# Layer 2 attention in steps of three score tiles and three quarter runs of values

## The chip, the core and the metric

The kernel runs on one core of a Trainium2 chip. A core has TensorE (matrix products into PSUM, the accumulator memory; the profile calls it PE and its weight loads PEld), VectorE (DVE), ScalarE (ACT), GpSimd (POOL) and SyncE (SP, which issues DMA transfers). Each engine takes its instructions in a fixed order, and semaphores make one engine wait for another. So the order that is built into the program decides who waits for whom. The metric is the device time of one execution in microseconds (us).

## The reference

Four layers, each an attention over a context and a feed-forward part, act on x of shape 4 x 256 x 256 (batch, tokens, width). Layer 2's attention is the part that matters here. It has 16 query heads of 128, four heads to each of 4 key/value groups, and keys of two origins: 1601 context keys and the 256 tokens themselves, the latter under a causal mask.

```
q = (x @ wq).reshape(B, L, NUM_HEADS, HEAD_DIM)
k = (x @ wk)...; v = (x @ wv)...            # 4 groups, repeated for their 4 heads
k_ctx = rms_norm(h_ctx_kv @ wk_ctx ...); v_ctx = h_ctx_kv @ wv_ctx ...
q, k = rms_norm + rotary embedding
scores = jnp.einsum('blhd,bmhd->bhlm', q, k_full) * scale + mask
probs = jax.nn.softmax(scores, axis=-1)
out = jnp.einsum('bhlm,bmhd->blhd', probs, v_full)
return out.reshape(B, L, NUM_HEADS * HEAD_DIM) @ wo
```

## The kernel before

**Units, heads, tiles.** `l2_xattn` (L1361) works through 16 units, one for each batch and key/value group, with 4 heads in each: 64 heads. The context's keys and values were projected earlier and are loaded for each unit (`prep`, L1452). A head's 256 queries are cut into 8 groups of 32, and two groups make a score tile. So a head has four score tiles, c = 0 to 3, and the layer has 256.

**Scores** (`scores`, L1549). The stationary side is 32 queries, so four matmuls work side by side on quarters of the array (128x32 weights), each over a quarter of the keys; a tile has eight such fours, of 416, 448 or 480 columns (causality makes later groups longer). In the trace every fp32 matmul is two passes. The tile lies in PSUM in one of three buffers of two banks (`ps_s`, L1375). VectorE adds the mask and takes the row maximum, ScalarE takes the exponential with the row sum into an SBUF tile p (8 buffers, L1560).

**Softmax of a head.** A row's keys lie in four quarters of the partitions, each with its own maximum and sum. `merge` (L1578) gathers these (GpSimd, ms), forms shares on VectorE and ScalarE (lo, em, wm, tot), and GpSimd writes the factors (rm). `scale` (L1603) multiplies p by them with eight GpSimd instructions. `turn` (L1611) transposes p on VectorE into pT (two buffers), in blocks of 32.

**Values** (`values`, L1618). For each of 15 blocks of keys one matmul with full 128x128 weights adds into o (256 columns), and after the last block ScalarE copies o to `at` (L1627). o has one buffer (`ps_o`, L1377). `CHUNK` (L1638) cuts the 15 into runs of 4, 4, 4 and 3.

**Side work.** `prep` of the next unit is a generator whose pieces are: two query projections (tpq, two matmuls of 512 columns each, read by ScalarE's square and VectorE's two products), keys and values of the tokens (tpkv), the norm's factors (two loads of ScalarE's table), two rounds of transposes of the queries (tpqT) and one of the keys (tpk). `project` (L1629) multiplies a unit's four heads by wo (acc, 16 passes). tpq, tpkv, tpqT, tpk and acc share one PSUM buffer (`ps`, L1376).

**Order.** The loop at L1677 makes steps of two score tiles, eight to a unit. A step issues two tiles, a part of the previous head's softmax, and half of the values (two runs) of the head before that; the tables `WHEN` and `BETWEEN` (L1674, L1675) say how many pieces of `prep` go into each step, and `project` of the last unit comes in step 7. The tile framework's scheduler then sets the order of each engine's instructions, except those that `pin` (L165) keeps in the order of the program: the transposes and the first sum of a merge. `mm` (L116) calls `ordered`, which pins a matmul only while `self.strict` is set; in this layer it is not.

Of the kernel before, what the change touches and what calls it, by code (L numbers as in the profile page):

```python
# [11 lines left out]
F32 = mybir.dt.float32  # L12
# [6 lines left out]
AF = mybir.ActivationFunctionType  # L19
ALU = mybir.AluOpType  # L20
# [77 lines left out]
class Kernel:  # L98
# [1262 lines left out]
    def l2_xattn(self):  # L1361
# [10 lines left out]
        with ExitStack() as es:  # L1372
# [28 lines left out]
            def turned(b):  # L1401

                xn = self.xn.tile([P, 2, D], F32, name="xn")
                if b:
                    self.layernorm(xn, self.x[b])
                    exps_next()
                else:

                    mv = self.small.tile([P, 2, 2], F32, name="ln_mv")
                    for q in range(2):  # L1410
                        st = self.small.tile([P, 6], F32, name="st3")
                        nc.vector.bn_stats(st, self.x[b][:, q, :])
                        nc.vector.bn_aggr(mv[:, q, :], st)
                    r = self.small.tile([P, 8], F32, name="ln_r8", bufs=1)
                    self.root(r[:, :2], mv[:, :, 1], 1.0, 1e-5, r[:, 2:])
                    for q in range(2):
                        nc.vector.tensor_scalar(
                            xn[:, q, :], self.x[b][:, q, :], mv[:, q, 0:1], r[:, q : q + 1],
                            ALU.subtract, ALU.mult,
                        )  # L1420
                    self.fill(LN2)
                tp = ps.tile([P, 2, 2, P], F32, name="tp_ln", tag="tp")
                for k in range(2):
                    for q in range(2):
                        nc.tensor.transpose(tp[:, k, q, :], xn[:, q, k * P : (k + 1) * P], self.ident)
                t = self.xnT.tile([P, 2, S], F32, name="xT2", tag="xnT")
                nc.scalar.copy(t, tp.rearrange("p k q t -> p k (q t)"))
                return t
# [18 lines left out]
            def load_out(g):  # L1447
                t = two.tile([P, 4, D], F32, name="wo")
                nc.sync.dma_start(t, i["l2_wo"][g])
                return t  # L1450

            def prep(u, w, res):  # L1452
# [75 lines left out]
                    yield  # L1528
                tp = ps.tile([P, 4, P], F32, name="tpk", tag="tp")
                for m in range(2):  # L1530
                    nc.tensor.transpose(tp[:, m, :], ko[:, m, :], self.ident)
                c = CT * P + 96
                nc.gpsimd.memset(kT[:, NK - 1, 96:], 0.0)
                nc.scalar.copy(
# [11 lines left out]
                n0, n1 = tiles_of(2 * c), tiles_of(2 * c + 1)  # L1546
                return [(0, 2, n0)] if n0 == n1 else [(0, 1, n0), (1, 2, n1)]

            def scores(kT, qT, h, c, ms):  # L1549

                s = ps_s.tile([P, 2, 512], F32, name="s2")
                for n in range(2):
                    q0 = (2 * c + n) * 32
                    nt = tiles_of(2 * c + n)
                    for a in range(4):
                        self.mm(
                            s[32 * a : 32 * a + 32, n, : nt * 32].rearrange("p (t i) -> p t i", i=32),
                            qT[:, h, q0 : q0 + 32], kT[:, :nt, 32 * a : 32 * a + 32], True, True,
                        )
                p = main.tile([P, 2, NK * 32], F32, name="p2", bufs=8)  # L1560
                for n0, n1, nt in spans(c):
                    e0, e1 = 2 * c + n0, 2 * c + n1
                    sv = s[:, n0:n1, CT * 32 : nt * 32]
                    nc.vector.tensor_tensor(  # L1564
                        sv, sv, mask[:, e0:e1, : nt - CT, :].rearrange("p n t i -> p n (t i)"), ALU.add
                    )
                    nc.vector.tensor_reduce(  # L1567
                        ms[:, 0, e0:e1], s[:, n0:n1, : nt * 32], AX.X, ALU.max, negate=True
                    )
                    for n in range(n0, n1):  # L1570
                        e = 2 * c + n
                        nc.scalar.activation(  # L1572
                            p[:, n, : nt * 32], s[:, n, : nt * 32], AF.Exp, bias=ms[:, 0, e : e + 1],
                            accum_out=ms[:, 1, e : e + 1],
                        )
                return p

            def merge(ms):  # L1578

                c = self.small.tile([32, 4, 2, 8], F32, name="ms2")
                for a in range(4):
                    nc.gpsimd.tensor_copy(c[:, a], ms[32 * a : 32 * a + 32])
# [4 lines left out]
                e = self.small.tile([32, 4, 8], F32, name="em2")  # L1589
                nc.vector.tensor_tensor(e, wide(lo), c[:, :, 0], ALU.subtract)  # L1590
                nc.scalar.activation(e, e, AF.Exp)
                yield
                w = self.small.tile([32, 4, 8], F32, name="wm2")
                nc.vector.tensor_tensor(w, e, c[:, :, 1], ALU.mult)
                tot = self.small.tile([32, 8], F32, name="tot2")
# [4 lines left out]
                    nc.gpsimd.tensor_tensor(r[32 * a : 32 * a + 32], e[:, a], tot, ALU.mult)  # L1600
                return r

            def scale(p, r, c):  # L1603
                for n in range(2):
                    e = 2 * c + n
                    nt = tiles_of(e)
                    nc.gpsimd.tensor_scalar(  # L1607
                        p[:, n, : nt * 32], p[:, n, : nt * 32], r[:, e : e + 1], 1.0, ALU.mult, ALU.mult
                    )

            def turn(p, pT, c):  # L1611
                for n0, n1, nt in spans(c):
# [24 lines left out]
            ORDER = [0, 13, 14, *range(1, NM)]  # L1637
            CHUNK = [ORDER[0:4], ORDER[4:8], ORDER[8:12], ORDER[12:]]  # L1638

            def softmax_steps(hd):  # L1640


                shares = merge(hd["ms"])
                next(shares)
                yield
                r = yield from shares
                hd["pT"] = main.tile([P, 8, NK, 32], F32, name="pT2")
                for c in range(4):
                    scale(hd["p"][c], r, c)
                yield  # L1650
                for c in range(4):
                    turn(hd["p"][c], hd["pT"], c)
                yield

            def value_steps(hd):
                o = ps_o.tile([P, S], F32, name="o2")
                for n, ms in enumerate(CHUNK):
                    values(hd["va"], hd["pT"], hd["at"], hd["h"], o, ms)
                    if n % 2:
                        yield  # L1660

            units = [(b, g) for b in range(B) for g in range(NKV2)]
            w = load(0)
# [3 lines left out]
                self.fill(Q2 if n == 0 else C2 if n == 3 else 0)  # L1667
            for _ in self.early:
                pass
            self.es2.close()  # L1670
            main = es.enter_context(tc.tile_pool(name="a2main", bufs=2, side="right", reuse_waits="tile"))


            WHEN = [0, 1, 1, 1, 1, 1, 1, 0]  # L1674
            BETWEEN = [0, 0, 0, 0, 0, 0, 1, 0]  # L1675
            soft = vals = hd = None
            for n, (b, g) in enumerate(units):  # L1677
                kT, va, qT = ready
                last = hd
                ready, pieces = [], None  # L1680
                wo_now = wo
                at = main.tile([P, 4, S], F32, name="at2", bufs=2)
                for h in range(4):
                    hd = {"ms": self.small.tile([P, 2, 8], F32, name="nmsm2"), "p": [], "va": va, "at": at, "h": h, "b": b,
                          "wo": wo_now}
                    for c in (0, 2):
                        step = 2 * h + c // 2
                        for cc in (c, c + 1):
                            hd["p"].append(scores(kT, qT, h, cc, hd["ms"]))
                        if soft is not None:  # L1690
                            next(soft[0])
                        if pieces is not None:
                            for _ in range(BETWEEN[step]):
                                next(pieces, None)
                        if vals is not None:
                            next(vals)
                        if step == 0 and n + 1 < len(units):
                            b1, g1 = units[n + 1]
                            w = load(g1)
                            pieces = prep(n + 1, w, ready)  # L1700
                            if g1 == 0:
                                next(pieces)
                        if step == 4 and n + 1 < len(units):
                            wo = load_out(g1)
                        if pieces is not None:
                            for _ in range(WHEN[step]):
                                next(pieces, None)
                        if step == 7 and last is not None:
                            project(last)
                        if soft is not None and c == 0:  # L1710
                            next(soft[0])
                    vals = value_steps(soft[1]) if soft is not None else None
                    soft = (softmax_steps(hd), hd)
                if pieces is not None:
                    for _ in pieces:
                        pass
            for n in range(2):
                next(soft[0])
                next(vals)
                if n == 0:  # L1720
                    next(soft[0])
            for _ in value_steps(hd):
                pass
            project(hd)


    def l3_open(self, es):

# [759 lines left out]
```

## Time and profile before

| what | us |
|---|---|
| median of 3 runs (lowest, highest) | 2390.23 (2389.08, 2396.24) |
| the profiled execution | 2387.69 |
| its span, from first to last instruction | 2386.0 |
| layer 2 attention in it, first scores to end of the last projection | 691.1 to 1689.6 |
| all score matmuls of that layer, TensorE busy | 424.2 |
| all value matmuls of that layer, TensorE busy | 431.7 |

The profile's durations come from the one profiled execution, whose own time is 1.7 us over its span. Matmuls are pipelined: a row's mean duration is longer than the distance from one start to the next, so costs on TensorE are read from starts, or from the chain of waits, which gives each stretch its share of time without overlap. The columns of a group are: line, engine, operation, output <- inputs, shapes, count, then busy time and mean of one in ns, then the idle time of the engine just ahead of them and who ended it.

### The profile page before, as it was taken

The numbers are of one execution on the slowest core, as the hardware profiler recorded it, in microseconds if no ns is written. First come the engines' busy times: TensorE is split into PE (matmuls) and PEld (weight loads), VectorE is DVE, ScalarE is ACT, GpSimd is POOL, SyncE is SP. The second block draws the span as 40 slices with busy tenths as digits, with TensorE's granted clock in tenths as the row PEclk, the third lists the DMA queues.
The fourth block names the chain that finished last, engine by engine and source line by source line (L and its number), as shares of the span: only waits on it lengthen the run. The fifth ranks groups of instructions, "written<-read, shape, count | busy, mean of one in ns | idle before, by whom it ended". The sixth has DMA issues, their size and how long they took to land.

```text
span 2386.0 us, 42230 instructions
## 1 busy us (share of the span) xinstructions
PE 2255.6 (95%) x14335; PEld 1382.2 (58%) x14335; DVE 1473.2 (62%) x3553; ACT 1272.4 (53%) x2877; POOL 948.7 (40%) x1707
## 2 busy tenths in 40 slices
PE   8989997889989999999999999999899889999996
PEld 5677875777745555555555655555665533444332
DVE  5453532773457777777777777777334574758344
ACT  3334443552474555555555555553232577888994
POOL 1014655503335544555554555554121253334220
PEclk9989998989999999999999999999899999999998
DMA  7165575652550111111111111100534353434320
GB/s 267 41 201 161 172 156 157 197 185 65 167 179 32 43 51 47 47 51 51 51 52 51 51 51 50 44 10 10 205 124 117 114 156 103 109 94 103 83 64 19
DMA packets 156078, 234.47 MB, mean 98 GB/s; under 512 B 33929, under 2 KB 122761, under 8 KB 154666
## 3 DMA queue, kind: packets, MB, share of 16 engines
q1 hardware_dynamic: 138998, 190.07, 25.0%
q0 software_dynamic: 11280, 31.60, 5.4%
q10 hardware_dynamic: 5588, 10.09, 1.4%
q8 instruction: 117, 1.92, 0.3%
q14 instruction: 95, 0.78, 0.1%
HBM read 169.94 MB, written 61.74 MB: 97 GB/s over the span
## 4 chain that ended last, share of the span: by engine, by line
PE 78%; DVE 7%; issue 5%; DMA 4%; ACT 2%; POOL 2%; SPq 1%; ACTq 0%; POOLq 0%; DVEq 0%
PE o L117 17%; PE s L117 17%; PE o L77 6%; PE b L77 3%; PE f2gu L117 3%; PE s L77 3%; PE f1gu L117 2%; PE fill L1307 2%; PE f0gu L117 2%; PE acc L117 2%; PE tpq L117 2%; PE av L117 2%; PE f0y L117 2%; PE f2y L117 1%; PE f1y L117 1%
## 5 line engine op out<-in xcount | busy, mean ns | idle before, releaser
L1572 ACT ACTIVATE p<-s,nmsm 128x448 f32<-128x448 f32 (+2 forms) x512 | 324.7, 639 | 369.6 <-DVE nmsm L1567 317.4
L117 PE MATMUL o<-pT,va 128*128 128x256 f32 (+2 forms) x1920 | 431.7, 377 | 3.3 <-DVE pT L1613 2.9
L117 PE MATMUL s<-kT,qT 128*32 128x448 f32 (+2 forms) x4096 | 424.2, 550 | 4.2 <-ACT p L1572 4.2
L77 ACT ACTIVATE e<-s 128x1024 f32<-128x1024 f32 (+1 forms) x416 | 392.4, 1041 | 57.4 <-PE s L77 56.3
L117 PEld LDWEIGHTS o<-pT,va 128*128 128x128 f32 (+1 forms) x1920 | 344.7, 190 | 127.9 <-issue 75.4
L1607 POOL TENSOR_SCALAR p<-p,rm 128x448 f32<-128x448 f32 (+2 forms) x512 | 320.7, 649 | 6.3
L1567 DVE TENSOR_REDUCE nmsm<-s 128x1 f32<-128x448 f32 (+4 forms) x384 | 293.2, 783 | 4.4
L1613 DVE STREAM_TRANSPOSE pT<-p 128x448 f32<-128x448 f32 (+4 forms) x384 | 278.1, 778 | 11.1 <-POOL p L1607 11.1
L117 PEld LDWEIGHTS s<-kT,qT 128*32 128x32 f32 x4096 | 121.7, 109 | 250.2 <-issue 213.9
L77 PE MATMUL o<-e,va 128*32 128x512 f32 x1656 | 246.9, 614 | 12.3 <-DVE os L77 12.2
L1600 POOL TENSOR_TENSOR rm<-em,tot 32x8 f32<-32x8 f32 x256 | 50.3, 197 | 335.6 <-DVE tot L1597 303.3
L1564 DVE TENSOR_TENSOR s<-s,mask 128x64 f32<-128x64 f32 (+4 forms) x384 | 92.5, 260 | 128.5 <-PE s L117 82.4
L77 PEld LDWEIGHTS s<-qb,kb 32*128 32x128 f32 (+1 forms) x1664 | 65.5, 180 | 182.3 <-issue 143.7
L1307 PE MATMUL fill<-wkc_early,ctxT 128*128 128x256 f32 (+1 forms) x444 | 110.5, 401 | 8.9 <-ACT va_early L1315 6.7
L522 POOL DMA_INDIRECT f0xr<-f0xd,f0src x95 | 91.3, 961 | 66.5 <-PE f0y L117 25.5
L77 PE MATMUL s<-qb,kb 32*128 32x256 f32 (+1 forms) x1664 | 111.5, 331 | 3.1 <-ACT e L77 1.8
L77 POOL CAST kb<-kf 128x384 fp32r<-128x384 f32 (+1 forms) x126 | 65.5, 549 | 96.4 <-PE s L77 61.8
L1307 PEld LDWEIGHTS fill<-wkc_early,ctxT 128*128 128x128 f32 (+1 forms) x444 | 87.0, 200 | 25.3 <-ACT va_early L1315 7.8
L1572 ACT ACTIVATION_READ_ACCUMULATOR p<-s,nmsm 128x1 f32 x512 | 100.5, 196 | 0.0
L1326 DVE TENSOR_REDUCE ss_early<-sq_early 128x4 f32<-128x512 f32 x64 | 37.1, 580 | 82.8 <-ACT sq_early L1325 72.0
L630 POOL DMA_INDIRECT f0yt<-f0yd,f0slot x64 | 63.1, 987 | 60.7 <-DVE x L622 29.8
L117 PE MATMUL f2gu<-f2wgu,f2xsT 128*128 x176 | 85.1, 608 | 0.6 <-ACT f2xsT L114 0.3
(579 smaller groups left out, 3689.2 us busy)
## 6 DMA issues: line engine op xcount, KB each, us to landing
kf<-kd SPq DMA_DIRECT2D x384, 48.0 KB
vd<-va_early SPq DMA_DIRECT2D x96, 128.0 KB
kd<-kT_early SPq DMA_DIRECT2D x48, 256.0 KB
kT<-kd SPq DMA_DIRECT2D x16, 768.0 KB
va<-vd SPq DMA_DIRECT2D x16, 768.0 KB
kd<-kt SPq DMA_DIRECT2D x96, 128.0 KB
f0yd<-f0ys SPq DMA_DIRECT2D x95, 128.0 KB
ctxT<-in_ctxT SPq DMA_DIRECT2D x5, 1664.0 KB
```

The costliest lines, as they stand in the source:

```text
L77: ins = f(*a, **kw)
L117: self.ordered(self.nc.tensor.matmul(out, lhsT, rhs, start=start, stop=stop, **kw))
L522: nc.gpsimd.indirect_dma_start(out=t, out_offset=None, in_=xd[:, :], in_offset=bass.IndirectOffsetOnAxis(ap=src[:, n : n + 1], axis=0),)
L630: nc.gpsimd.indirect_dma_start(out=yt, out_offset=None, in_=yd[:, :], in_offset=bass.IndirectOffsetOnAxis(ap=slot[:, t, r : r + 1], axis=0),)
L1307: ins = nc.tensor.matmul(tp[:rows, t, :], ctxT[u // NKV2][:, k, c0 : c0 + rows], w[u % NKV2][:, k, :], start=k == 0, stop=k == 1,)
L1326: nc.vector.tensor_reduce(ss[:, m0:m1], sq[:, : m1 - m0, :], AX.X, ALU.add)
L1564: nc.vector.tensor_tensor(sv, sv, mask[:, e0:e1, : nt - CT, :].rearrange("p n t i -> p n (t i)"), ALU.add)
L1567: nc.vector.tensor_reduce(ms[:, 0, e0:e1], s[:, n0:n1, : nt * 32], AX.X, ALU.max, negate=True)
L1572: nc.scalar.activation(p[:, n, : nt * 32], s[:, n, : nt * 32], AF.Exp, bias=ms[:, 0, e : e + 1], accum_out=ms[:, 1, e : e + 1],)
L1600: nc.gpsimd.tensor_tensor(r[32 * a : 32 * a + 32], e[:, a], tot, ALU.mult)
L1607: nc.gpsimd.tensor_scalar(p[:, n, : nt * 32], p[:, n, : nt * 32], r[:, e : e + 1], 1.0, ALU.mult, ALU.mult)
L1613: self.pin(nc.vector.transpose(pT[:, 2 * c + n0 : 2 * c + n1, :nt, :].rearrange("p n t i -> p n (t i)"), p[:, n0:n1, : nt * 32],))
```

## The change

The loop over units, heads and pairs of tiles becomes one flat loop over the 256 score tiles, three to a step. Tile x belongs to unit x // 16 and head x // 4; k = x % 16 is its place in the unit.

- A step first issues the scores of three tiles; mask, maximum and exponential are a function of their own (`weights`), called for the first two tiles, and for the third after the first run of values.
- Then follow three positions. Position x issues a quarter run of the values that lies nine tiles back (`LATE` = 9), and then `beside`, the side work of that place: `PIECES` puts tpq at k = 0 and 4, tpkv at 6, the norm at 7, tpqT at 10 and 12, tpk at 13; `project` is at k = 8, the loads of wo at 9 and of the next but one unit's wq and wks at 13.
- Heads whose last tile was in the step have merge and scaling issued at its end, and their transposes after the first run of values of the next step.
- `self.strict` is set for the loop, so TensorE keeps the order of the program; transposes tp_ln and tpk are ordered too.
- p has 9 buffers instead of 8. The last head's scaling is shared between GpSimd and ScalarE.

What is computed does not change, nor do the number and shapes of the matmuls.

```diff
-            def scores(kT, qT, h, c, ms):
+            def scores(kT, qT, h, c):
...
+                return s
+
+            def weights(s, c, ms):
+
+                p = main.tile([P, 2, NK * 32], F32, name="p2", bufs=9)
...
-            def scale(p, r, c):
+            def scale(p, r, c, shared):
                 for n in range(2):
                     e = 2 * c + n
                     nt = tiles_of(e)
+                    v = p[:, n, : nt * 32]
+                    if shared and n:
+                        nc.scalar.activation(v, v, AF.Copy, scale=r[:, e : e + 1])
+                    else:
+                        nc.gpsimd.tensor_scalar(v, v, r[:, e : e + 1], 1.0, ALU.mult, ALU.mult)
...
+            w = load(1)
...
-            WHEN = [0, 1, 1, 1, 1, 1, 1, 0]
-            BETWEEN = [0, 0, 0, 0, 0, 0, 1, 0]
...
+            PIECES = {0: 1, 4: 1, 6: 1, 7: 1, 10: 1, 12: 1, 13: 9}
+            heads, turning, pieces = [], [], None
...
+            def beside(n, k):
+
+                nonlocal w, wo, pieces
+                if k == 8 and n:
+                    project(heads[4 * n - 1])
+                if n + 1 == len(units):
+                    return
+                b1, g1 = units[n + 1]
+                if k == 0:
+                    pieces = prep(n + 1, w, ready)
+                for _ in range(1 if k == 2 and g1 == 0 else PIECES.get(k, 0)):
+                    next(pieces, None)
+                if k == 9:
+                    wo = load_out(g1)
+                if k == 13 and n + 2 < len(units):
+                    w = load(units[n + 2][1])
...
+            self.strict = True
+            LATE, ALL = 9, 16 * len(units)
+            for i0 in range(0, ALL + LATE, 3):
+                run = range(i0, min(i0 + 3, ALL))
+                made = []
+                for x in run:
+                    n, h, c = x // 16, x // 4 % 4, x % 4
+                    if x % 16 == 0:
+                        begin(n)
+                    hd = heads[x // 4]
+                    if c == 0:
+                        hd["ms"] = self.small.tile([P, 2, 8], F32, name="nmsm2")
+                    made.append((hd, c, scores(hd["kT"], hd["qT"], h, c)))
...
+                soften(slice(0, 2))
+                for pos in range(3):
+                    x = i0 + pos
+                    if LATE <= x < ALL + LATE:
+                        value_chunk(heads[(x - LATE) // 4], (x - LATE) % 4)
+                    if pos == 0:
+                        soften(slice(2, 3))
+                    if x < ALL:
+                        beside(x // 16, x % 16)
+                    if pos == 0:
+                        for hd in turning:
+                            turns(hd)
+                        turning = []
+                for hd, c, _ in made:
+                    if c == 3:
+                        softmax(hd, hd is heads[-1] and len(heads) == 4 * len(units))
+                        turning.append(hd)
+            project(heads[-1])
+            self.strict = False
```

## The prediction

> **What bounds the kernel now.** I read the page first, then the busy time of the engines over three stretches of the layer 2 attention, then the chain inside one unit of it, then the rows of its side engines.
>
> ```profile
> span 2386.0 us, 42230 instructions
> PE 2255.6 (95%) x14335; PEld 1382.2 (58%) x14335; DVE 1473.2 (62%) x3553; ACT 1272.4 (53%) x2877; POOL 948.7 (40%) x1707
> ```
> ```profile
> core 0: us, PE busy (x) PEld busy (x) DVE busy (x) ACT busy (x) POOL busy (x), PEclk, DMA share, GB/s
> 691.07:718.95 27.88, 23.66 (x183) 7.23 (x182) 21.42 (x48) 19.91 (x50) 10.33 (x24) 0.93 0.24 83
> 718.95:1663.60 944.65, 943.87 (x6383) 552.34 (x6382) 728.80 (x1582) 489.58 (x1364) 485.88 (x1083) 1.00 0.13 44
> 1663.60:1689.60 26.00, 23.37 (x109) 19.50 (x106) 12.50 (x22) 3.64 (x12) 10.25 (x22) 1.00 0.00 1
> ```
>
> From 718.95 us (first values) to 1663.60 (last scores) TensorE is idle for 0.8 us of 945, at a granted clock of 1.00. Layer 2 attention is bound by TensorE's own queue; VectorE is next with 77%, ScalarE has 52%, GpSimd 51%. The page's chain gives values and scores 17% of the span each. What TensorE does inside one unit:
>
> ```profile
> 1029.34 3.31 PE s L117 x32
> 1032.65 3.22 PE o L117 x14
> 1035.87 0.44 PE tpqT L1526 x4
> 1036.30 3.09 PE s L117 x32
> 1039.39 0.59 PE tpqT L1526 x4
> 1039.98 0.03 issue
> 1040.02 3.46 PE o L117 x16
> 1043.48 0.22 PE tpk L1531 x2
> 1043.70 3.30 PE s L117 x32
> 1047.00 3.22 PE o L117 x14
> 1050.22 3.45 PE acc L117 x16
> ```
>
> (start, length, work; a matmul is two passes.) Read three things. The 16 passes of acc take 3.45 us, 0.216 each, so 14 value passes should take 3.02; after scores they take 3.22. Second, the second tpqT takes 0.59 where the first took 0.44, then 0.03 and a slower run: TensorE waits for the transposes pT of VectorE, about 0.27 us a unit. Third, a unit repeats every 62.0 us (the same tpqT stands at 977.35 and 1039.32). The rows that take part in the new steps:
>
> ```profile
> L1572 ACT ACTIVATE p<-s,nmsm 128x448 f32<-128x448 f32 (+2 forms) x512 | 324.7, 639 | 369.6 <-DVE nmsm L1567 317.4
> L1607 POOL TENSOR_SCALAR p<-p,rm 128x448 f32<-128x448 f32 (+2 forms) x512 | 320.7, 649 | 6.3
> L1567 DVE TENSOR_REDUCE nmsm<-s 128x1 f32<-128x448 f32 (+4 forms) x384 | 293.2, 783 | 4.4
> L1613 DVE STREAM_TRANSPOSE pT<-p 128x448 f32<-128x448 f32 (+4 forms) x384 | 278.1, 778 | 11.1 <-POOL p L1607 11.1
> ```
> ```profile
> L1627 ACT COPY at<-o x64: 366/370/378, 729.0 to 1686.7; 128x256 f32<-128x256 f32 x64
> ```
>
> The last one empties the only value buffer (min/median/max ns). Today nothing on TensorE waits for it: a score block of 3.1 us stands between a head's last values and the next head's first.
>
> **The change, part by part.** The order of instructions on each engine is read from the two programs, every time from the rows.
>
> *Fewer changes between scores and values (gain).* The same 2048 score and 960 value matmuls are issued. Blocks of scores fall from 126 to 86; after the first values, from 123 to 82. One round trip costs, by starts in the trace: the pass ahead of scores 0.309 instead of 0.216 (tpq at 1004.53 to scores at 1006.34: 1.81 for four passes that the chain gives 1.72); the first four scores 0.02 more; the last four 0.49 to 0.51 instead of 0.376 to 0.403; the first value pass 0.320. Together 0.33. 41 x 0.33 = 13.5 us. All of it is on the path, since TensorE has no gaps.
>
> *The wait of tpqT for pT (gain).* In the new order a head's first values come with its transposes several us old. 14 units x 0.27 = 4 us.
>
> *Start and end.* Before the first values there are now 12 tiles (96 score matmuls) instead of 85, and both tpq. Up to the fourth tile the orders agree; then qo and qt (0.68 each) stand ahead of tile 3 on VectorE, so head 0's sums come 1.5 to 3 us later, and the first values at about 720. For that 11 more score matmuls (2.1 us) and 1.7 us of tpq lie before them, which the old kernel did ahead of 691 while idle. Net gain 1 us, bounds -3 to +4. At the end the old kernel has 23.0 us of TensorE work after the last score in 26.0; the new one 19.4 us of work, with the last head's scaling shared (8 x 0.63 becomes 4 x 0.65 on GpSimd beside four on ScalarE). After the last score: mask and max 1.7, two exponentials 1.3 with gaps, sums to shares 3.6 (the old row chain 1667.6 to 1673.8 less its wait), scaling and transposes to about 12.5; then 6.45 of values and 3.5 of projection: 22.4, idle 3 as before. Nothing.
>
> *Steady supply.* SP's queue issues the same loads; wq and wks one unit earlier, DMA share is 0.13, so nothing. Scores wait for three buffers: a tile's two exponentials must end within the 11.2 us of a step; VectorE's three tiles take 4.7, so even 3 us late they do. The ninth p tile covers the later turn. Values start two steps after their head's last tile, 27 us against about 17 to 21 for sums, scaling (1.0 + 5.0) and transposes (4.3). No stall from these.
>
> *The value buffer (loss).* This is the wait that the change adds. A head's last quarter run now falls at places 0, 4, 8 and 12 of a unit, followed at once by tpq (1.72), tpq, acc, and tpqT (0.44); then comes the next head's first run into the same buffer. acc's fourth matmul, 1.30 us in, reads the copy itself. The copy stands in ScalarE's queue behind exponentials of the same step: four of them where the place is first in its step, six where it is second; where it is last, the next step's scores (4.7 us) cover it. Queued behind a waiting TensorE is everything on it.
>
> One place worked out: place 4 of every third unit (score tiles 36 to 38). VectorE comes to that step late. In the step before (tiles 33 to 35, 9.8 us: scores 4.8, runs 1.5 + 1.73 + 1.73), it finishes tpq's reads at 2.6 (ss 0.66, qo, qt 0.68 after ScalarE's square 0.60), the merge's sums at 6.1 behind tile 35's max; GpSimd's shares and scaling take 6.05, to 12.25; the sixth transpose 1.15 more: 13.4, or 3.6 us into the next step. There follow merge, four max rows and masks (0.2, 0.5, 1.0, 0.55 and the small ones): the second max of tile 36 ends at 7.8, its exponential at 8.5, the copy at 8.9, and with the hand-over about 9.1. TensorE has scores 4.7, the run 1.40 and tpq 1.72 behind it at 7.8. Wait 1.3, plus 0.1 for the slow first pass: 1.4.
>
> The same walk at the other places, each five times: place 8 of that unit, behind the norm's two table loads (1.28 each) and six exponentials, copy ready at 10.6 against 9.3: 1.4. Place 8 of the next phase, same cause with four exponentials: 1.2. Place 12: tpqT covers only 0.44: 0.7 where first, 0.4 where second. Sum 5.1 x 5 = 25.5. Two units where the layer norm's four transposes stand instead of tpq, and three bare hand-overs in the last unit (no side work, 0.8 each): 3.5. Bounds: below, nothing but the last unit, 3; above, every copy 0.5 later at 25 places, 42. I take 29, since the walk's terms are rows.
>
> A page of the Trainium skill speaks against this change: Trace Analysis, Optimizing Tensor Performance (Matmuls), wants independent groups to rotate through different PSUM banks, so that emptying one overlaps the next. By the rule alone all 64 hand-overs would pay copy and hand-over, about 0.7 each, 45 us. The row of 370 ns says that an idle ScalarE would be hidden by tpq or acc; so the queue ahead of the copy decides, not the single buffer.
>
> **Sum.** -13.5 - 4 - 1 + 29 = +10.5. The profiled execution took 2387.7 (span 2386.0, 1.7 around it), so 2398; it is 0.1% under the median 2390.2. I forecast 2399.
>
> **Rivals.**
> *Copies come in time (faster).* If ScalarE's queue stands 1.3 us earlier at these places, only 3 us are lost: -18.5 + 3 = -15.5, 2375. For it: ScalarE is busy 52% only and its wait row shows it mostly waiting for VectorE's max. Against: those waits are what delays the copy. It decides below 0.95 us of wait a unit.
> *Half the waits.* 14.5 lost, 18.5 won: 2386, with bounds 2382 to 2393. For it: the walk's terms add up over two steps, and 0.6 less on each copy is 6% of that way.
> *Score buffers run out.* If VectorE falls over 5 us behind in its heaviest steps (transposes, tpq's reads and three tiles: 11.8 us of work in a step of 11.2), the next step's scores wait too; 1 us in each third of 86 steps is 28 us more: 2427. Against: the following step has no transposes.
> *The price of a change of mode is a wait's price.* Then 13.5 is not won: 2412. Against: 0.495 and 0.320 come in every block alike, with the semaphore 0.6 or 5.5 us old.
>
> **How the numbers follow.** 0.3% (7 us) is about what can be told from no change. My forecast (2393 to 2412) 0.47, copies in time 0.24, half the waits 0.20, the last two 0.09. Faster takes 0.24 with a little of the half case, 0.25; same the rest of it and my forecast's lower edge, 0.26; slower 0.49. The range leaves out about one in ten on each side: 2375 to 2416; my case alone 2393 to 2412.
>
> **What would show it.** Score rows x48 with 86 blocks; a unit of 60.7 us of TensorE work plus gaps. Gaps ahead of o named "ACT at", near 1 us, 25 to 35 in all, and at acc; no tpqT waiting for pT. Wrong if those gaps are under 0.4 us, or if gaps stand ahead of s.

## The result and the profile after

The changed kernel took 2417.6 us (median of four runs, 2413.5 to 2418.3) beside 2391.4 for the kernel before (2389.1 to 2396.2): a ratio of 1.0104, with a 95% interval of 1.0084 to 1.0123. It is slower, by 26 us where I had forecast 9, and 1.6 us above the top of my range. The head of its page and the three stretches of the attention (first scores, first values, last scores, end), with the columns of the stretches as before:

```profile
span 2416.6 us, 42176 instructions
PE 2252.9 (93%) x14335; PEld 1388.8 (57%) x14335; DVE 1490.1 (62%) x3553; ACT 1276.4 (53%) x2881; POOL 947.8 (39%) x1703
```
```profile
core 0: us, PE busy (x) PEld busy (x) DVE busy (x) ACT busy (x) POOL busy (x), PEclk, DMA share, GB/s
694.41:723.28 28.87, 26.13 (x210) 8.41 (x209) 22.28 (x47) 18.85 (x49) 10.82 (x24) 0.97 0.25 85
723.28:1694.60 971.32, 939.38 (x6377) 557.89 (x6377) 751.24 (x1595) 492.43 (x1368) 491.88 (x1089) 1.00 0.13 42
1694.60:1717.00 22.40, 19.63 (x94) 16.49 (x90) 7.48 (x15) 5.04 (x12) 4.03 (x12) 1.00 0.00 1
```

In the middle stretch TensorE was idle for 0.8 us before; now it is idle for 32. Who ended the waits of TensorE from 723.3 to 1717 (us in total, times, longest):

```profile
PE acc L117 <- ACT at L1629: 17.4, 10, 3.4
PE o L117 <- ACT at L1629: 14.0, 20, 1.3
PE o L117 <- DVE pT L1615: 2.5, 2, 1.8
PE s L117 <- ACT p L1576: 0.5, 1, 0.5
```

The copy of o into `at` is what TensorE waits for, and almost nothing stands ahead of s. A wait also costs something behind it, so I counted lost time from the starts in the trace: each distance between two starts beyond what that pair takes undisturbed (0.216 us for a pass of 256 columns, 0.429 for 512, 0.109 for a transpose, 0.39 for four score passes side by side, and the prediction's surcharges at a change of work), where it is over 0.02. (A score tile is eight matmuls, that is 16 passes in four such fours; the "eight such fours" of the section on the kernel before should read so.) In the attention:

| | before | after | difference | forecast |
|---|---|---|---|---|
| first scores to last acc pass | 998.1 | 1021.9 | +23.8 | +10.5 |
| lost time in it | 19.9 | 57.3 | +37.4 | |
| of that, first values to last scores | 7.5 | 48.0 | +40.5 | +29 - 4 |
| of that, start and end | 12.4 | 9.3 | -3.1 | -1 |
| the rest: work without lost time | 978.2 | 964.6 | -13.6 | -13.5 |

The two profiles differ by 6.8 us more outside the attention (the medians, 26 apart, leave some 2.5 for that). The tpkv of the first unit, up to which every engine's order is the same, already starts at 675.21 instead of 671.87, so I don't count it to the change. These 2.5 us are more than the 1.6 by which the time passed my range: the 23.8 of the attention alone would have ended just inside it. Lost time by place, as the sum over the units that have it (five each, four where place 8 is third), with the passes slowed behind it:

| place | forecast | after | norm behind copy | copy two earlier, held | both | acc at 11 |
|---|---|---|---|---|---|---|
| 4, first in step | 7.0 | 5.8 | 5.6 | 0 | 0 | 5.9 |
| 8, second in step | 7.0 | 8.2 | 0 | 7.7 | 0 | 17.2 |
| 8, first in step | 6.0 | 14.1 | 20.3 | 3.6 | 0.6 | 17.8 |
| 8, third in step | 0 | 1.2 | 0.9 | 0 | 0 | 0 |
| 12, first in step | 3.5 | 3.0 | 3.7 | 2.6 | 2.6 | 10.8 |
| 12, second in step | 2.0 | 3.1 | 2.3 | 1.0 | 1.0 | 1.0 |

With the layer-norm places and the last unit (4.9, forecast 3.5) the changed kernel loses 40 where I had 29. The bare waits named "ACT at", 31.4 in all, lie inside the 25 to 35 that the prediction said would show; most of the rest is the slow passes at and behind them. The columns on the right belong to the experiments. One row is far off: place 8 first in its step. It looks like this in unit 1 (start, length, engine, operation, and in brackets the idle time ahead of it); first TensorE, then ScalarE, then VectorE (here and below, the short accumulator read after each of ScalarE's exponentials is left out):

```profile
779.37 1.56 PE L117 MATMUL o<-pT,va 128*128 128x256 f32 x6
780.77 1.46 PE L117 MATMUL acc<-wo,at 128*128 128x256 f32 x6
783.95 2.43 PE L117 MATMUL acc<-wo,at 128*128 128x256 f32 x10 [1.72 <-ACT at L1629]
```
```profile
776.56 1.28 ACT L125 ACT_TABLE_LOAD   x1
779.01 0.30 ACT L125 ACTIVATE ss<-ss,eps 128x10 f32<-128x10 f32 x1 [1.18 <-DVE ss L1510]
779.34 1.28 ACT L1432 ACT_TABLE_LOAD   x1
...
781.56 0.61 ACT L1576 ACTIVATE p<-s,nmsm 128x416 f32<-128x416 f32 x1
782.30 0.63 ACT L1576 ACTIVATE p<-s,nmsm 128x448 f32<-128x448 f32 x1
782.92 0.62 ACT L1576 ACTIVATE p<-s,nmsm 128x448 f32<-128x448 f32 x1
783.53 0.37 ACT L1629 COPY at<-o 128x256 f32<-128x256 f32 x1
```
```profile
776.76 1.18 DVE L1615 STREAM_TRANSPOSE pT<-p 128x960 f32<-128x960 f32 x1 [0.35 <-POOL p L1611]
777.87 0.79 DVE L1506 TENSOR_TENSOR kt<-kr,l_knwrb 128x256 f32<-128x256 f32 x1
...
779.12 0.59 DVE L1571 TENSOR_REDUCE nmsm<-s 128x1 f32<-128x416 f32 x1
...
780.26 0.94 DVE L1591 TENSOR_TENSOR em<-lo,ms 32x32 f32<-32x32 f32 x1
781.13 1.07 DVE L1571 TENSOR_REDUCE nmsm<-s 128x2 f32<-128x896 f32 x1
```

The last values are issued by 780.8; acc's seventh pass, which reads the copy, could start at 782.1. The copy stands behind the norm's two table loads with an idle 1.18 between them, and behind three exponentials. The last two of those read a maximum that VectorE finishes only at 782.2, because it comes late from the transposes. The two are level: the first exponential, straight behind the loads, ends at 782.17 and that maximum at 782.20. Which of the two holds the copy can't be read from here, so it was tried.

### The profile page after: what moved, and what is told of

It reads as the page before. It is cut to its first block, busy times and chain, and to the rows that moved or that the text cites. A ratio compares the mean times of both kernels' runs of the same rounds, so it can differ in the third digit from the quotient of the medians.

```text
span 2416.6 us, 42176 instructions
## 1 busy us (share of the span) xinstructions
PE 2252.9 (93%) x14335; PEld 1388.8 (57%) x14335; DVE 1490.1 (62%) x3553; ACT 1276.4 (53%) x2881; POOL 947.8 (39%) x1703
## 5 line engine op out<-in xcount | busy, mean ns | idle before, releaser
L117 PE MATMUL s<-kT,qT 128*32 128x448 f32 (+2 forms) x4096 | 411.0, 549 | 2.6 <-ACT p L1576 2.6
L1611 POOL TENSOR_SCALAR p<-p,rm 128x416 f32<-128x416 f32 x508 | 317.9, 649 | 6.3
L1592 ACT ACTIVATE em<-em 32x32 f32<-32x32 f32 x64 | 14.5, 227 | 145.8 <-DVE em L1591 145.8
L1487 POOL TENSOR_TENSOR qo<-qo,qt 128x512 f32<-128x512 f32 x32 | 41.2, 1287 | 126.6 <-DVE lo L1589 92.7
L1585 POOL COPY ms<-nmsm 32x16 f32<-32x16 f32 x256 | 48.3, 189 | 108.2 <-ACT p L1576 93.6
```

The lines of the kernel that those rows point to most:

```text
L117: self.ordered(self.nc.tensor.matmul(out, lhsT, rhs, start=start, stop=stop, **kw))
L1487: nc.gpsimd.tensor_tensor(o1, o1, t2, ALU.add)
L1611: nc.gpsimd.tensor_scalar(v, v, r[:, e : e + 1], 1.0, ALU.mult, ALU.mult)
```

## The experiments

The experiments ran where the kernel before took 2341 to 2344 us; there the attention begins at 643 to 654 us instead of 691. So I compare ratios to the kernel before in the same batch, and in the traces the distance from the first value pass to the last: 967.3 us before, 989.56 after in the first profile and 989.52 in a repeat. All edits are to the changed kernel. TensorE's order in the layer is the changed kernel's in runs 1 to 9 and 11. But in all of them except 11 the scheduler also moved instructions of VectorE, and in most of GpSimd, that the edit doesn't name, so a run changes more than its diff shows.

**1. No copy.**

```diff
-                if ms[-1] == CT:
-                    nc.scalar.copy(at[:, h, :], o)
...
-                at = main.tile([P, 4, S], F32, name="at2", bufs=2)
+                at = still
```

> The changed kernel without the copy of o into at: at is one tile, filled once ahead of the loop, so the last projections multiply constants (that part of the computation is left out; every score, value and projection matmul is still there). Theory (the waits for the copy are what is lost): the 31.4 us of waits named 'ACT at L1629' and about 5 us of slow passes behind them go: 2417.6 - 36 = 2381, between 2376 and 2387, and no other wait of over 3 us takes their place. Rival (another engine is late at these places, and the copy is only the last to be named): its wait shows instead, ahead of o or acc, and the time stays above 2400. Rival (fewer changes between scores and values bring nothing): about 2390 or more, equal to the kernel before, although the waits are gone.

Ratio 0.998 (0.9969 to 0.9992); first to last value pass 958.2, which is 31.3 less than after and 9.1 less than before. The waits for the copy are gone. I had expected 36 less, with no other wait of over 3 us in their place; there are tpkv 4.9 in four and pT 3.6 in two (2.5 in two before the edit). Lost time in the attention is 27.3 instead of 57.3, and the work without it again 964.6. So the waits for the copy hold the loss, and the 13.6 us of fewer changes are real. Both rivals fall, the second by the work without lost time: the time itself is only 0.2% under the kernel before.

**2. to 4. The order on ScalarE.** Run 2 pins exponentials and copies in program order; run 3 also issues exponentials one position later (mask and maximum stay); run 4 issues the third tile's ahead of the first run.

```diff
-                        nc.scalar.activation(
+                        self.pin(nc.scalar.activation(        # runs 2, 3, 4
...
+                    if pos < 2:                               # run 3
+                        exps_of(slice(pos + 1, pos + 2))
...
-                soften(slice(0, 2))
+                soften(slice(0, 3))                           # run 4
```

> Control for the next two: the exponentials and the copies are held on ScalarE in the order in which the program issues them, which is nearly the order that they have in the changed kernel. Each theory expects the changed kernel's time, 2417.6, within 4.

> The same order held, but each tile's two exponentials are issued one position later, so the copy of a run that is first in its step stands behind two exponentials in place of four, and of one that is second behind four in place of six. Nothing is left out. Theory (the queue ahead of the copy sets the wait): each wait falls by up to two exponentials, 1.3 us: place 4 by 1.3, place 8 first in step by 1.3 of 1.9, place 8 second in step by 1.25, place 12 by 0.6 and 0.5, each five times, and the same in the last unit: 27 us less, 2390, between 2384 and 2397. Rival (the buffer's own hand-over, matmul to copy to matmul, sets the wait): under 5 us less, 2413 or more. Rival (the exponentials that now come later leave the scores waiting for a buffer): the waits ahead of o fall, but waits ahead of s of 10 us and more appear: 2400 to 2412.

> The opposite: the third tile's mask, maximum and exponentials are issued ahead of the first run of values too, and the order is held, so a copy first in its step stands behind six exponentials in place of four (at place 4 behind the square of tpq as well, at place 12 behind the copy of tpqT). Nothing is left out. Theory (queue): place 4 +1.9, place 8 +1.3, place 12 +1.9, place 0 +0.5, each five times: 28 us more, 2446, between 2433 and 2453. Rival (own hand-over): within 5 of 2417.6.

Ratios 1.0489 (1.0468 to 1.0511), 1.0081 (1.0062 to 1.0100) and 1.0692 (1.0674 to 1.0710); first to last value pass 1070.1, 983.8 and 1132.1. The control was none: holding the order cost 80 us. `pin` holds an instruction behind the one that the program issued last on its engine, so a tile's second exponential can no longer let the copy pass. Unit 1, place 8, in run 2:

```profile
749.52 0.61 ACT L1576 ACTIVATE p<-s,nmsm 128x416 f32<-128x416 f32 x1
751.50 0.63 ACT L1576 ACTIVATE p<-s,nmsm 128x448 f32<-128x448 f32 x1 [1.28 <-DVE nmsm L1571]
752.13 0.62 ACT L1576 ACTIVATE p<-s,nmsm 128x448 f32<-128x448 f32 x1
752.74 0.63 ACT L1576 ACTIVATE p<-s,nmsm 128x448 f32<-128x448 f32 x1
753.35 0.38 ACT L1629 COPY at<-o 128x256 f32<-128x256 f32 x1
```

Four exponentials instead of three, and the second waits 1.28 for its maximum. acc waits 5.3 there instead of 1.9: counted from the first scores of the step (741.11, and 774.72 in the changed kernel), the copy starts after 12.2 us instead of 8.8. Of these 3.4, 1.6 are there before the first exponential starts (8.4 instead of 6.8), and 1.9 are the one exponential more: its own 0.6 and the 1.28 that it waits for its maximum. From run 2, two exponentials fewer are worth 86 us and two more cost 62, in the direction of the queue theory, at twice to three times the size that I gave. In run 3 places 4 and 12 lost their waits as expected, but the copies at place 8 third in the step came to stand behind the pinned norm: 21.5 us in four units. Pins were the wrong tool; the next runs hold only what is to be held.

**5. to 8. Two causes apart.** Run 5 holds behind the copy, in issue order only, all that the program issues on ScalarE after it in that step. Run 6 also moves the norm from place 7 to 8. Run 7 is run 5 with exponentials one position later; run 8 has both.

```diff
+                            behind.enter_context(tc.issue_after(copy))
...
-            PIECES = {0: 1, 4: 1, 6: 1, 7: 1, 10: 1, 12: 1, 13: 9}
+            PIECES = {0: 1, 4: 1, 6: 1, 8: 1, 10: 1, 12: 1, 13: 9}      # runs 6, 8
...
+                        if pos < 2:                                     # runs 7, 8
+                            exps_of(slice(pos + 1, pos + 2))
```

> Control: in each step, what the program issues on ScalarE after the copy is held behind the copy (issue order only), and nothing else is held. The copy stands where it stood, behind three to six exponentials and at place 8 behind the norm's two table loads. Only the layer norm's table loads of a new batch move behind a copy. From the first value pass to the last (989.6 us in the changed kernel's profile, 967.4 in the kernel before) each theory expects 986 to 992; waits named 'ACT at' stay at 28 to 34.

> As the control, and the norm piece of the side work is issued at place 8 in place of 7, behind the copy: its square, its two table loads (1.28 each) and the idle 1.18 between them, in which ScalarE waits for VectorE's sum, no longer stand ahead of the copy. Theory (at place 8 it is the norm on ScalarE's queue that made the wait larger than I had worked out): place 8's waits fall from 14.1 (first in step), 8.2 (second) and 1.2 (third) to under 6 together; acc almost leaves the list of waits; places 4 and 12 stay (5.8 and 7.1). tpqT at place 10 may wait up to 1 us for qo, five times. First to last value pass 973, between 967 and 980. Rival (only the exponentials ahead of the copy count): place 8 falls by less than 3 us in all, 985 or more.

> As the control, and each tile's two exponentials are issued one position later, so that the copy stands behind two fewer; the norm stays at place 7. Theory (queue): places 4 and 12 lose all their waits (5.5 and 6), place 8 loses 0.6 to 1.3 each where first and 1.3 where second in its step, 11 in all: 22 less, 968, between 962 and 976, and the waits that are left stand at place 8. Rival (the later exponentials keep score buffers or transposes waiting): waits ahead of s or for pT of 8 us and more, 976 or above.

> Both edits together: the copy behind two exponentials fewer, and the norm behind the copy. Theory: no wait named 'ACT at' of over 0.7 us is left, the sum under 6; first to last value pass 959, between 955 and 965 (958.2 without any copy), which is 4 to 12 less than the kernel before, and the time of an execution 0.995 to 0.9995 of the kernel before. Rival (waits move to the next thing that is late: tpqT for qo, scores for their buffers): 966 or more, not faster than the kernel before.

Ratios 1.0150 (1.0123 to 1.0176), 1.0151 (1.0128 to 1.0174), 1.0074 (1.0050 to 1.0097) and 1.0013 (1.0002 to 1.0024); first to last value pass 1003.3, 1004.9, 985.1 and 974.5. Run 5 missed its 986 to 992 for a reason of my making: the layer norm of a new batch stands at place 0 and was held too, and its transposes now waited for it in three units, in runs 6 to 8 as well:

```profile
PE tp_ln L1425 <- DVE xn L160: 11.1, 3, 4.2
```

By place the four still tell most of the causes apart (table above; run 5 itself has 5.9, 9.6, 12.6, 1.2, 2.9 and 2.3 in the table's order, near the changed kernel's). *Norm behind the copy:* place 8 second in its step falls from 8.2 to 0, as expected. But where place 8 is first the loss grows from 14.1 to 20.3, against my theory. In all, place 8 gains 2.3, and run 6 missed its 967 to 980: this is the rival's figure. VectorE (first fence) and ScalarE at that place in unit 1 of run 6:

```profile
726.28 0.15 DVE L1589 TENSOR_REDUCE lo<-ms 32x8 f32<-32x32 f32 x1
...
728.55 0.59 DVE L1571 TENSOR_REDUCE nmsm<-s 128x1 f32<-128x416 f32 x1
...
730.13 1.61 DVE L1571 TENSOR_REDUCE nmsm<-s 128x2 f32<-128x896 f32 x2
```
```profile
729.26 0.61 ACT L1576 ACTIVATE p<-s,nmsm 128x416 f32<-128x416 f32 x1 [1.85 <-DVE nmsm L1571]
731.33 0.63 ACT L1576 ACTIVATE p<-s,nmsm 128x448 f32<-128x448 f32 x1 [1.37 <-DVE nmsm L1571]
731.96 0.63 ACT L1576 ACTIVATE p<-s,nmsm 128x448 f32<-128x448 f32 x1
732.56 0.63 ACT L1576 ACTIVATE p<-s,nmsm 128x448 f32<-128x448 f32 x1
733.17 0.38 ACT L1629 COPY at<-o 128x256 f32<-128x256 f32 x1
```

No table load is near, and ScalarE waits for the maxima all the same. The head's merge (lo, em, wm, tot) now runs ahead of the first maximum, and four exponentials stand ahead of the copy. *Copy two earlier:* place 4 loses all of its loss, place 12 most of it in all units but the first and the last, and place 8 first falls to 3.6 with the norm left where it was; place 8 second keeps 7.7. With the layer norm's wait in it, run 7 takes 18 less than run 5 where I had 22. So the norm's loads hold the copy where place 8 is second in its step, and late exponentials hold it at places 4 and 12. At place 8 first neither run parts the two cleanly. In run 6 the merge came ahead of the maxima. In run 7 the norm's chain itself came earlier (in unit 1 the first exponential starts at 734.46, 5.5 us after the step's first scores instead of 6.8), and the 3.6 that are left all stand in unit 7, behind the loads. With both edits, no unit but the first and the last loses more than 0.3 us to the copy. Run 8 as a whole still missed its 955 to 965, by the layer norm's waits (10.9 us).

**9. to 12. Only what matters held, and three more.** Run 9 is run 8, but holds only the later exponentials and, at place 8, the norm. Run 10 is run 9 with tpkv at place 7. Run 11 is the changed kernel again; run 12 is that kernel with acc at place 11.

```diff
+                    if pos < 2:                                         # runs 9, 10
+                        with held():
+                            exps_of(slice(pos + 1, pos + 2))
...
+                        with held(x % 16 == 8):
...
-                if k == 8 and n:
+                if k == 11 and n:                                       # run 12
```

> As the run with both edits, but only two things are held behind a copy: the exponentials of later positions of its step, and the norm at place 8. The layer norm of a new batch at place 0 floats again as in the changed kernel, so TensorE's 14.0 us of waiting for it (places 0 of units 3, 7 and 11) should go. Theory (the waits for the copy were the whole loss): first to last value pass 974.5 - 14.0 = 960.4, between 957 and 964, beside 967.3 in the kernel before; time of an execution 0.994 to 0.999 of the kernel before. Rival (something else is late where the copy no longer is): 966 or more, 1.000 or above.

> The run before, and tpkv moves from place 6 to 7, where in every third unit it comes after the next step's scores and so after the reads of tpq. Theory: the 3.4 us of waits ahead of tpkv go, place 8 second in its step gains up to 0.8 each (the copies of tpkv now stand ahead of the copy of o): between 957 and 964, within 3 of the run before. Rival: tpqT waits for qo by over 1 us at each of five places, 965 or more.

> The changed kernel itself beside the others of this batch. First to last value pass 986 to 992 (989.6 in its first profile) wherever the stages outside this layer stand; 1.008 to 1.013 of the kernel before.

> The changed kernel with the projection (acc) at place 11 in place of 8. Nothing then stands on TensorE between a head's last run at place 8 and the next head's first run into o. Theory (the copy's place on ScalarE sets the time, and acc's first three matmuls hide 1.30 of it): the waits at place 8, first and second in the step, move from acc to o and grow by 1.3 each, ten times, and some of them, over 2.7 long, bring passes at half rate behind them as the one of 3.5 us did: first to last value pass 1003, between 997 and 1012. Rival (only acc, which reads the fresh copy, is hurt): its 20 us go, 968 to 974.

Run 9: ratio 0.9960 (0.9947 to 0.9973), 2334.9 us beside 2344.3, first to last value pass 958.5, as expected. It is faster than both kernels, than the one before by 0.4%. Two rows of TensorE's waits in it, and its middle stretch:

```profile
PE o L117 <- ACT at L1633: 4.0, 6, 1.7
PE tpkv L117 <- issue: 2.8, 4, 0.7
```
```profile
679.01:1619.03 940.02, 933.10 (x6376) 558.05 (x6376) 771.96 (x1595) 488.45 (x1368) 490.47 (x1089) 1.00 0.14 44
```

Of 31.4 us of waits for the copy 4.0 are left, nearly all in the first unit and the last. Run 10 missed: ratio 1.0022 (1.0012 to 1.0032), 972.9. The waits ahead of tpkv went, but acc shares tpkv's PSUM buffer and now waited until ScalarE had read that:

```profile
PE acc L117 <- ACT va L1497: 12.9, 9, 2.2
```

Run 11: ratio 1.0115 (1.0100 to 1.0130), 989.5, as expected. Run 12: ratio 1.0290 (1.0271 to 1.0309), 1031.3, far above even my 1012. The waits at place 8 moved from acc to o (52.0 us in 24 waits) and grew by 1.2 where first (unit 1: 1.99 to 3.15) and by 2.0 where second (1.35 to 3.30), so the rival falls. What I had too small is what follows: some 110 value passes behind these waits lost some 21 us (some 30 passes and 3.4 us in the changed kernel), and place 12 first in its step went from 3.0 to 10.8.

## Why the prediction was wrong, point by point

**What bounds the kernel.** Right: TensorE's own queue; the 22.2 us between first and last value pass are waits of TensorE minus work saved.

**Fewer changes between scores and values, -13.5.** Right: 86 blocks, and -13.6 once lost time is taken out, in both the changed kernel and run 1. The price per round trip held, so the rival *price of a change of mode is a wait's price* falls.

**The wait of tpqT for pT, -4.** Right: tpqT never waits for pT after; its one wait, 0.3 us, is for qo.

**Start and end, -1.** A gain of 3.1, near the upper of the bounds (-3 to +4). The two walks themselves came out: the first values start 28.9 us after the first scores, as forecast (691 to about 720), and from the last scores to the end it takes 22.4 as forecast.

**Steady supply.** Nearly right: 0.5 us of waits ahead of s from the first values on, so *score buffers run out* falls. *Half the waits* falls too, with 40 lost instead of 14.5.

**The value buffer, +29.** This is the step that failed. The mechanism was right (run 1 without the copy and run 9 with it moved both take nearly all of these waits away) and its size was not: 40 by place, and with smaller losses beside them (tpkv 1.2 and many under 0.2) the lost time of the middle stretch grew by 40.5 where the prediction had 29 - 4. The term that was mis-sized is "place 8 of the next phase, same cause with four exponentials: 1.2". It measured 2.0 to 2.1 in four units and 5.8 in unit 7, 14.1 instead of 6.0. So 8.1 of the 11 us too little come from this one term, 4.6 of them from unit 7 alone. "Same cause" was the error: the walk that I made for place 4, from VectorE's late transposes to the last maximum ahead of the copy, I did not make here, but took over the norm's loads from the place before. In the trace of unit 1 the loads and the late maximum end level here, and in unit 7 a fourth exponential stands ahead of the copy. How the 2.0 us divide between loads and exponentials stays open, since runs 6 and 7 moved VectorE's instructions too.

The other terms are near: place 4 has 1.37 to 1.38 in four units against 1.4, place 12 first 0.62 against 0.7 in three of four units and second 0.46 against 0.4 in four of five, place 8 second 1.35 against 1.4 in four of five. But for place 4, the one place worked out, part of that is luck. In unit 2 its step begins with scores at 821.89 (VectorE first, then ScalarE):

```profile
825.23 1.18 DVE L1615 STREAM_TRANSPOSE pT<-p 128x960 f32<-128x960 f32 x1 [0.35 <-POOL p L1611]
...
827.54 1.09 DVE L1571 TENSOR_REDUCE nmsm<-s 128x2 f32<-128x896 f32 x1
```
```profile
828.75 0.64 ACT L1576 ACTIVATE p<-s,nmsm 128x448 f32<-128x448 f32 x1 [0.72 <-DVE tot L1597]
...
830.60 0.38 ACT L1629 COPY at<-o 128x256 f32<-128x256 f32 x1
```

The transposes end 4.5 us into the step where the walk had 3.6, and the last maximum ahead of the copy at 6.7 instead of 7.8. After it ScalarE runs three exponentials, not one, so that the copy ends at 9.1 where I had 8.9: errors that nearly cancel.

**The bounds.** "Above, every copy 0.5 later at 25 places, 42" was about what came, but not for its reason: it was a bound on the sum of equal small errors, and the error was mostly one place, with a slowed clock on top in unit 7.

**The rival *copies come in time*, 2375.** It did not happen in the changed kernel, but run 9 is near it: ScalarE's queue freed at these places, and 9 us won instead of 15, since 24.2 us of lost time remain in its attention (tpkv 3.4, start, first unit and end) where the rival had 3 in the middle stretch.

## What to carry to other kernels

In these runs a copy that empties a single buffer cost what stood ahead of it on its engine's queue, and that was not only the durations of those instructions but also the latest input that any of them waited for. Follow that chain (here GpSimd's scaling, VectorE's transposes and maxima, ScalarE's exponentials) at every place by itself; two places that look alike (place 8 second and first in its step) answered differently to the same edit. When such a wait shows, first reorder the emptying engine: issuing two exponentials and a norm behind the copy instead of ahead of it turned 1.0115 into 0.9960 with no change in TensorE's order (VectorE's moved along).

## What the runs showed of the hardware that I had not expected

A long wait of TensorE was paid twice. In unit 7 the wait at place 8 was 3.4 us (four exponentials ahead of the copy instead of three), and this is the busy time around it, with the granted clock as the third last number:

```profile
1150.00:1160.00 10.00, 10.00 (x69) 6.97 (x72) 8.92 (x18) 7.76 (x20) 7.08 (x18) 1.00 0.10 26
1160.00:1167.50 7.50, 4.28 (x28) 2.46 (x20) 6.45 (x18) 5.42 (x16) 4.49 (x9) 0.96 0.35 114
1167.50:1173.50 6.00, 5.84 (x14) 4.73 (x15) 2.09 (x5) 1.49 (x5) 4.51 (x8) 0.50 0.01 4
```

For 6 us TensorE was granted half its clock, and eleven passes came at 0.427 instead of 0.216. I counted the waits of TensorE (idle time ahead of a matmul, from the first value pass to the last) over the profiles of all twelve runs and the first one, leaving out those ahead of transposes. Among the next 15 passes some came at 0.38 to 0.46 after 14 of 62 waits of 1.3 to 2.6 us, after 10 of 11 of 2.6 to 3.0, after 17 of 21 of 3.0 to 4.0, and after 26 of 26 longer ones. The Trainium skill, page "TensorE: Matmul & The Clock Gate", section "HAM oscillation — how this bites in real kernels", says that gaps of more than about 3.4 us bring TensorE back to half rate. These runs agree with the half rate; waits somewhat shorter had it too. It fits that run 12 and the pinned runs 2 and 4 grew by more than their waits did: from the first values to the last scores their granted clock was 0.97, 0.97 and 0.94 on average, 1.00 in the changed kernel.
